# Moving one sequence's Mamba prologue from the FFN in front of its scan into the scan of the sequence ahead

## The chip, the cores and the metric

The kernel runs on one core of a Trainium2 chip. Its engines work side by side, each through its own queue of instructions in order: TensorE (PE: matmuls and transposes, with PEld for its weight loads), VectorE (DVE), ScalarE (ACT: activation functions and copies), GpSimd (POOL) and SyncE (SP: it issues most of the transfers). The metric is the time of one execution on the device, in microseconds (us).

## The reference

Sixteen sequences (B = 16) of S = 512 tokens with D = 256 channels, in float32, go through four layers with residuals: a Mamba-like selective scan, an FFN with FP4-quantized operands, a causal linear attention, and the same FFN again. Each layer sees a layernorm of its input.

```python
x = L0_attn_a_x                                                     # (16, 512, 256)
x = x + mamba(layernorm(x), w_in, w_x, w_dt, b_dt, A_log, Dp)
x = x + ffn(layernorm(x), w_gate, w_up, w_down)                     # FP4 in blocks of 16
x = x + linear_attention(layernorm(x), W_attn, b_attn, W_proj, b_proj)
x = x + ffn(layernorm(x), w_gate, w_up, w_down)

# mamba, cut to what matters
x_in = x @ w_in                                                     # u
dt_low, Bm, Cm = split(x_in @ w_x, [64, 80])
dt = softplus(dt_low @ w_dt + b_dt) * (DT_MAX - DT_MIN) + DT_MIN
A = -exp(A_log)                                                     # (256, 16)
def step(h, (dtt, ut, bt, ct)):                                     # over 512 tokens
    dA = dtt[:, :, None] * A
    inp_term = einsum('bdn,bn,bd->bn', dA, bt, ut)                  # the same for all d
    h = exp(dA) * h + inp_term[:, None, :]                          # h: (b, 256, 16)
    y = einsum('bdn,bn->bd', h, ct) + Dp * ut
```

The input term of the recurrence doesn't depend on the channel d. The state has 256 x 16 rows over 512 tokens for each sequence.

## The kernel before

**Sequences and layers.** Each sequence `b` passes through Python generators that emit instructions and yield after each piece an estimate of its length: `front` (L430), `prologue` (L444), `mamba` (L500), `ffn` (L571), `attention` (L649), `ffn` again. `weave` (L829) puts pieces of two generators side by side; `by_turns` (L867) takes from several so that each keeps to its share of a total.

**The Mamba layer.** `front` takes the layernorm's statistics of x (`bn_stats`, `bn_aggr` on VectorE, a power on POOL) and turns x to features on partitions: eight matmuls against a diagonal of the inverse deviations (L421, `pt_m`; each fp32 matmul stands as two in the profile, so sixteen), copied by ScalarE to `tT_m`. `prologue` makes everything that the scan needs, by matmuls of 128x512 from `tT_m`, four of them in the profile (two `k` steps, two records each) for each 128x512 result:

- `pz` (two halves) through Abs and Relu, then Tanh and Ln over the whole (L460 to L470) and one VectorE instruction (L471) to `dt`. Eight transfers (L476) write `dt` to DRAM as `dd`.
- `pu` (two halves), copied to `u`.
- `pcm`, copied to `cm` (C, each row repeated over eight channels).
- `dtu` = `dt` x `u` (VectorE, L485), two matmul steps to `pg` (L488); `pbm` (B) copied to one half of `inp` (L494), times `pg` (L495, VectorE), and copied to the other half (L496).

Buffers are tagged, and a tile waits until the tile before it with the same tag is read for the last time. `soft`, `dtu` and later the scan's result `yT` share one buffer (tag `soft`); `dt` and `inp` share one (tag `dt`); `u` and `cm` have one each.

`mamba` runs sixteen steps, each for two groups of 8 channels x 16 states. In a step: a transfer repeats rows of `dd` over the states (`sp`, L509, three buffers, issued two steps ahead); ScalarE makes the decay as Exp at half scale and a Square (`bar`, L521 and L524, two buffers, one step ahead); VectorE runs the scan over 2 x 512 elements (L540) and multiplies by `cm` (L544) to `h` (three buffers); PE sums over the states into `py` (L550, one PSUM bank in a pool of its own), where the skip term has been put at steps 1 and 9 (L538, from `u`). After steps 8 and 16 ScalarE copies `py` to `yT` (L555). At the end transposes and additions bring the result into x (L564, L377).

**FFN and attention.** The FFN quantizes its input on VectorE (L230 to L252), does two matmuls against resident weights (L592), the activation (L598 to L600), quantizes again in four chunks, transposes (L614) and multiplies (L627). Attention makes q and k through Exp and Relu (L670 to L672), and then in four chunks scores (L710, L717) and the products. `ko` (L681) is a copy of all of k with the even heads zeroed; each chunk's odd heads read from it.

**The order of the work.** For each round `b` from 1 to 15, the first half emits, by turns, `first(b)` up to FIRST = 76 units, and the second FFN of sequence `b - 2` with the beginning of attention `b - 1`. The second half emits the rest of `first(b)` by turns with the rest of attention `b - 1`. `first(b)` is the scan of `b`, with the front of `b + 1` from the seventh step on, and then FFN 1 of `b` with the prologue of `b + 1` among its pieces. So the last of a prologue is emitted at the end of a first half, and the scan that needs it in the next round.

The order of emission is not yet the order on the engines. The framework plans, at build time, each engine's order: emission order is the priority, and an instruction whose inputs and buffers are ready may go ahead of an earlier one that isn't. In the trace, steps of the scan of `b + 1` stand between pieces of FFN 1 of `b` that were emitted before them. All seven PSUM banks of the pool `bank` serve everything but `py`.

Of the kernel before, what the change touches and what calls it, by code (L numbers as in the profile page):

```python
# [32 lines left out]
def kernel(  # L33
# [63 lines left out]
    xs = [load(0)]  # L97
    begun, turned, stats = {}, {}, {}
    w_in_sb = const.tile([P, ND, D], F32, name="w_in_sb")
# [343 lines left out]

    def prologue(b):  # L444

        xnT = turned.pop(b)

        def from_xn(w, name):
            p = bank(f"{name}_{b}")
            for k in range(ND):  # L450
                nc.tensor.matmul(p, w[:, k], xnT[:, k, :], start=(k == 0), stop=(k == ND - 1))
            return p
# [11 lines left out]
        yield 0.5  # L464
        u = one.tile([P, ND, S], F32, tag="u", name=f"u_{b}")
        for e in range(ND):
            nc.scalar.copy(u[:, e, :], from_xn(w_in_sb[:, :, ts(e, P)], f"pu{e}"))
        yield 0.5
        nc.scalar.activation(soft, soft, AF.Tanh, scale=0.5)
# [9 lines left out]
        yield 1.5  # L479
        cm = one.tile([P, S], F32, tag="cm", name=f"cm_{b}")  # L480
        nc.scalar.copy(cm, from_xn(w_c_sb, "pcm"))


        dtu = one.tile([P, ND, S], F32, tag="soft", name=f"dtu_{b}")
        nc.vector.tensor_tensor(dtu, dt, u, ALU.mult)  # L485
        pg = bank(f"pg_{b}")
        for k in range(ND):
            nc.tensor.matmul(  # L488
                pg, a_rep[:, k].rearrange("p n i -> p (n i)"), dtu[:, k, :],
                start=(k == 0), stop=(k == ND - 1),  # L490
            )
        pb = from_xn(w_b_sb, "pbm")
        inp = one.tile([P, 2, S], F32, tag="dt", name=f"inp_{b}")
        nc.scalar.copy(inp[:, 0, :], pb)  # L494
        nc.vector.tensor_tensor(inp[:, 1, :], inp[:, 0, :], pg, ALU.mult)  # L495
        nc.scalar.copy(inp[:, 0, :], inp[:, 1, :])  # L496
        begun[b] = (u, dd, inp, cm)
        yield 2.5

    def mamba(b, xt):  # L500
        u, dd, inp, cm = begun.pop(b)

        yT = one.tile([P, ND, S], F32, tag="soft", name=f"yT_{b}")

# [25 lines left out]
        for at, (e, j, q0) in enumerate(steps):  # L530
# [5 lines left out]
            if j == 0 and q0 == 0:  # L536
                py = ps_y.tile([P, S], F32, tag="y", name=f"py_{b}_{e}")
                nc.tensor.matmul(py, d_diag[:, e], u[:, e, :], start=True, stop=False)  # L538
            h = one.tile([P, 2, S], F32, tag="hs", name=f"h_{b}_{e}_{j}_{q0}", bufs=3)
            nc.vector.tensor_tensor_scan(  # L540
# [6 lines left out]
            else:  # L547

                for q in range(4):
# [3 lines left out]
                    )  # L553
            if j == 3 and q0 == 2:
                nc.scalar.copy(yT[:, e, :], py)  # L555
            yield 3.5
# [92 lines left out]
    def attention(b, xt):  # L649
# [28 lines left out]


        ko = att.tile([P, ND, S], F32, tag="ko", name=f"ko_{b}", bufs=1)  # L680
        nc.scalar.activation(ko, kf, AF.Copy, scale=odd_heads[:, 0:1])  # L681
        yield 0.1

        def scores(c):
# [18 lines left out]
            yield 0.1  # L703

            psc = [bank(f"psc_{b}_{c}_{g}") for g in range(4)]
            for s in range(NH // 4):
                e, odd = divmod(s, 2)
                for g in range(4):
                    rows = slice(32 * g, 32 * g + (2 * HD if odd else HD))
                    nc.tensor.matmul(  # L710
                        psc[g][:, ts(s, P)], (ko if odd else kf)[rows, e, tok],
                        qf[rows, e, tok], start=True, stop=True,
                    )
# [13 lines left out]
        def attend(c, vp, sm):  # L727
# [21 lines left out]

            dx = att.tile([P, ND * HB, HD], F32, tag="dx", name=f"dx_{b}_{c}")  # L750
            nc.gpsimd.tensor_copy(
# [10 lines left out]
            if c < NC - 1:  # L762
                pk = bank(f"pk_{b}_{c}")
                for e in range(ND):
                    nc.tensor.transpose(pk[:, ts(e, P)], kf[:, e, tok], ident)
                kt = att.tile([P, D], F32, tag="kt", name=f"kt_{b}_{c}")
                nc.scalar.copy(kt, pk[:, :D])
# [69 lines left out]

    def first(b, scanned=False):

        if b + 1 < B:  # L840
            xs.append(load(b + 1))
        more = b + 1 < B
        fr = front(b + 1, xs[b + 1]) if more else iter(())
        if not scanned:
            yield from weave(mamba(b, xs[b]), fr, 6)
        yield from fr
        yield from weave(ffn(0, "f", b, xs[b]), prologue(b + 1) if more else iter(()), 0)

# [5 lines left out]

    FIRST, CHUNKS, FRONT, ATTN, FFN2 = 76.0, 30.0, 4.15, 23.0, 40.0

# [22 lines left out]
    with tc.tile_pool(name="prep", bufs=3) as prep, tc.tile_pool(name="prep_m", bufs=1) as prep_m:  # L879
        weights = ffn_weights(prep)  # L880
        next(weights)
        composite_weights(prep_m)
        for _ in weave(front(0, xs[0]), weights, 1, False):
            pass
        for _ in weave(prologue(0), weights, 0, False):
            pass
        for _ in weave(mamba(0, xs[0]), weights, 0):
            pass
    att = ctx.enter_context(tc.tile_pool(name="att", bufs=2))
    acts.append(ctx.enter_context(tc.tile_pool(name="act1", bufs=1)))  # L890
    by_turns([(first(0, True), CHUNKS)])
    for b in range(1, B):
# [40 lines left out]
```

## Time and profile before

The median of three runs is 2849.44 us (2849.22 to 2851.41). All below is of one profiled execution.

| | |
|---|---|
| profiled execution, its own time | 2856.84 us |
| its span, first to last instruction | 2855.1 us |
| mean granted TensorE clock | 0.929 of full |
| first scan instruction of sequences 1, 2, 3, 4 | 148.4, 260.1, 442.6, 610.6 us |
| rounds from sequence 3 to 15 | 167.3 to 170.6 us each |
| from the first to the last scan of one sequence, rounds 4 to 14 | 104 to 107 us |
| last scan instruction of sequence 15 ends | 2571 us |
| VectorE: scans and multiplies of the Mamba layer | 581.6 + 310.7 us |
| PE: reducing matmuls of the Mamba layer | 284.7 us |
| share of the 16 DMA engines, main queue | 22.0% |

Rounds repeat almost to the nanosecond from sequence 3 on, so one of them can be read for all. A table of stretches gives, for each stretch, the busy time of every engine; what an engine lacks to the length of the stretch is its idle time. The waits name who stood still, at which line, and what ended the wait. The chain of waits goes back from the last instruction to what released each one; what lies on it sets the time, and work that lies beside it costs nothing.

### The profile page before, as it was taken

The numbers are of one execution on the slowest core, as the hardware profiler recorded it, in microseconds if no ns is written. First come the engines' busy times: TensorE is split into PE (matmuls) and PEld (weight loads), VectorE is DVE, ScalarE is ACT, GpSimd is POOL, SyncE is SP. The second block draws the span as 40 slices with busy tenths as digits, with TensorE's granted clock in tenths as the row PEclk, the third lists the DMA queues.
The fourth block names the chain that finished last, engine by engine and source line by source line (L and its number), as shares of the span: only waits on it lengthen the run. The fifth ranks groups of instructions, "written<-read, shape, count | busy, mean of one in ns | idle before, by whom it ended". The sixth has DMA issues, their size and how long they took to land.

```text
span 2855.1 us, 34186 instructions
## 1 busy us (share of the span) xinstructions
PE 2450.1 (86%) x12907; PEld 1451.0 (51%) x12907; DVE 2433.6 (85%) x3545; ACT 1493.4 (52%) x2798; POOL 154.6 (5%) x153
## 2 busy tenths in 40 slices
PE   6577989898988889898898989989898888988997
PEld 3143555454554545455554545545455454545664
DVE  7797888989798898979888898888979889897565
ACT  4666455555545555554555555555554555553322
POOL 2000000000000000000000000000000000000000
PEclk7788999999999999999999999999899999999988
DMA  5332104132230313213031320403222041320000
GB/s 146 89 96 74 52 1 106 36 82 60 56 73 13 102 39 82 60 38 89 15 96 45 82 60 9 110 23 85 56 59 74 8 103 38 74 59 7 2 1 15
DMA packets 64376, 165.26 MB, mean 58 GB/s; under 512 B 8434, under 2 KB 26836, under 8 KB 64212
## 3 DMA queue, kind: packets, MB, share of 16 engines
q1 hardware_dynamic: 62592, 162.03, 22.0%
q8 instruction: 101, 1.65, 0.2%
q10 hardware_dynamic: 1620, 1.06, 0.1%
q14 instruction: 63, 0.52, 0.1%
HBM read 146.28 MB, written 16.78 MB: 57 GB/s over the span
## 4 chain that ended last, share of the span: by engine, by line
DVE 45%; PE 38%; ACT 8%; issue 6%; POOL 2%; DMA 0%; SPq 0%; ACTq 0%; DVEq 0%; POOLq 0%
DVE h L540 15%; PE po_g L627 5%; DVE h L544 5%; PE pg_g L592 4%; PE pu_g L592 4%; PE pqk L664 3%; DVE sm L717 3%; PE po_f L627 3%; PE pu_f L592 2%; PE pg_f L592 2%; DVE amax_f L230 2%; PE py L550 2%; DVE v_f L244 2%; DVE h_f L600 2%; DVE x L377 1%
## 5 line engine op out<-in xcount | busy, mean ns | idle before, releaser
L540 DVE TENSOR_TENSOR_SCAN h<-bar,inp 128x1024 f32<-128x1024 f32 x256 | 581.6, 2281 | 31.8 <-ACT inp L496 22.4
L521 ACT ACTIVATE bar<-sp,a_col 128x511 f32<-128x511 f32 x512 | 348.6, 715 | 287.6 <-DVE h L540 278.9
L550 PE MATMUL py<-h,red 128*32 128x512 f32 x1024 | 284.7, 712 | 111.6 <-DVE h L544 111.6
L544 DVE TENSOR_TENSOR h<-h,cm 128x1024 f32<-128x1024 f32 x256 | 310.7, 1214 | 1.0
L524 ACT ACTIVATE bar<-bar 128x1022 f32<-128x1022 f32 x256 | 269.8, 1054 | 5.6
L627 PE MATMUL po_f<-wdT,hqT_f 128*128 128x256 f32 (+1 forms) x768 | 205.8, 412 | 24.8 <-ACT hqT_f L618 24.8
L627 PE MATMUL po_g<-wdT,hqT_g 128*128 128x256 f32 (+1 forms) x768 | 200.1, 403 | 31.4 <-ACT hqT_g L618 31.4
L627 PEld LDWEIGHTS po_f<-wdT,hqT_f 128*128 128x128 f32 (+1 forms) x768 | 142.7, 199 | 120.3 <-ACT hqT_f L618 61.3
L592 PE MATMUL pg_f<-wgT,tT_f 128*128 128x352 f32 x512 | 191.3, 498 | 12.8 <-DVE sm L717 9.5
L592 PE MATMUL pu_f<-wuT,tT_f 128*128 128x352 f32 x512 | 178.5, 472 | 18.7 <-DVE sm L717 18.4
L627 PEld LDWEIGHTS po_g<-wdT,hqT_g 128*128 128x128 f32 (+1 forms) x768 | 138.6, 193 | 92.0 <-ACT hqT_g L618 45.2
L592 PE MATMUL pg_g<-wgT,tT_g 128*128 128x352 f32 x512 | 178.3, 471 | 0.0
L592 PE MATMUL pu_g<-wuT,tT_g 128*128 128x352 f32 x512 | 173.2, 460 | 0.0
L717 DVE TENSOR_TENSOR sm<-psc,causal 128x512 f32<-128x512 f32 x256 | 162.9, 676 | 5.4 <-PE psc L710 4.1
L248 ACT ACTIVATE big_f<-v_f 128x704 bf16<-128x704 f32 (+1 forms) x80 | 67.4, 842 | 166.9 <-DVE v_f L244 166.3
L592 PEld LDWEIGHTS pu_f<-wuT,tT_f 128*128 128x128 f32 x512 | 99.2, 196 | 80.9 <-DVE sm L717 25.7
L550 PEld LDWEIGHTS py<-h,red 128*32 128x32 f32 x1024 | 35.7, 116 | 203.6 <-DVE h L544 171.1
L592 PEld LDWEIGHTS pg_g<-wgT,tT_g 128*128 128x128 f32 x512 | 94.9, 191 | 73.4 <-issue 33.4
L592 PEld LDWEIGHTS pg_f<-wgT,tT_f 128*128 128x128 f32 x512 | 92.8, 197 | 76.1 <-issue 17.7
L592 PEld LDWEIGHTS pu_g<-wuT,tT_g 128*128 128x128 f32 x512 | 97.8, 191 | 54.7 <-issue 1.0
L664 PE MATMUL pqk<-tT_a,w_qkv_sb 128*128 128x512 f32 x256 | 125.1, 617 | 0.0
L598 ACT ACTIVATE h_g<-pg_g 128x352 f32<-128x352 f32 x128 | 59.0, 461 | 95.6 <-PE pg_g L592 94.8
(235 smaller groups left out, 4614.7 us busy)
## 6 DMA issues: line engine op xcount, KB each, us to landing
sp<-dd SPq DMA_DIRECT2D x256, 512.0 KB, 4.7
x<-in_L_attn_a_x_dram SPq DMA_DIRECT2D x16, 512.0 KB, 5.0
dd<-dt SPq DMA_DIRECT2D x128, 64.0 KB, 1.7
out_dram<-x SPq DMA_DIRECT2D x16, 512.0 KB, 4.5
w_qkv_sb<-in_L_attn_b_W_attn_dram ACTq DMA_DIRECT2D x1, 768.0 KB, 7.2
raw_d<-in_L_ffn_w_down_dram SPq DMA_DIRECT2D x1, 704.0 KB
raw_g<-in_L_ffn_w_gate_dram SPq DMA_DIRECT2D x1, 640.0 KB, 7.2
raw_u<-in_L_ffn_w_up_dram SPq DMA_DIRECT2D x1, 640.0 KB, 6.5
```

What stands on the lines that cost most here:

```text
L230: nc.vector.tensor_reduce(amax, src.rearrange("p (b k) -> p b k", k=BLK), AX.X, ALU.max, apply_absolute_value=True,)
L248: nc.scalar.activation(big, v, AF.Abs, scale=STEP)
L521: nc.scalar.activation(bar[:, i, 1:S], sp[:, i, 1:S], AF.Exp, scale=a_col[:, g : g + 1])
L524: nc.scalar.activation(bar[:, :, 1:S], bar[:, :, 1:S], AF.Square)
L540: nc.vector.tensor_tensor_scan(h.rearrange("p i t -> p (i t)"), bar.rearrange("p i t -> p (i t)"), inp.rearrange("p i t -> p (i t)"), 0.0, ...
L544: nc.vector.tensor_tensor(h, h, cm.unsqueeze(1).to_broadcast([P, 2, S]), ALU.mult)
L550: nc.tensor.matmul(py[32 * q : 32 * q + 32, :], red[:, j, :], (h0, h)[q // 2][:, q % 2, :], start=False, stop=(j == 3),)
L592: nc.tensor.matmul(pw[:, :HF], xqT[:, k, ts(c, P)], wT[:, k, cols], start=(k == 0), stop=(k == ND - 1),)
L598: nc.scalar.activation(hc, pg[:, :HF], AF.Tanh, scale=0.5)
L627: nc.tensor.matmul(po[:, :D], hqT[:rows, r, :], wdT[:rows, r, :], start=(r == 0), stop=(r == NR - 1),)
L664: nc.tensor.matmul(pz, w_qkv_sb[:, k, ts(je, P)], xnT[:, k, :], start=(k == 0), stop=(k == ND - 1),)
L717: nc.vector.tensor_tensor(t, psc[g].rearrange("p (s t) -> p s t", t=P), causal.unsqueeze(1).to_broadcast([P, NH // 4, P]), ALU.mult,)
```

## The change

- `prologue(b + 1)` now begins with `front(b + 1)`, and both are emitted among the steps of the scan of `b` (from its second step on) in place of the FFN. What follows the scan in `first(b)` is FFN 1 alone. The startup does the same with sequences 0 and 1.
- Within `prologue`, `pu` and `u` move behind `cm`. From there on it emits nothing until the scan ahead has emitted step 9, whose matmul is the last reader of `u` (the counter `halfway`).
- `dtu` is gone: `dt` is multiplied by `u` in place. B goes into `dt`'s first half (`term`), times `pg` there.
- `inp` has a buffer of its own. `mamba` fills it at its beginning: one half by ScalarE, one by POOL. Before, ScalarE wrote both within the prologue.
- `cm` has two buffers. `yT` is taken from the `soft` buffer only after step 8.
- In attention `ko` is made for each chunk (128x256 four times instead of 128x1024 once), and `dx` and `kt` have one buffer instead of two.
- The units FIRST and FRONT become 74.0 and 4.1.

```diff
-    def prologue(b):
-
+    def prologue(b, xt):
+
+        yield from front(b, xt)
         xnT = turned.pop(b)
...
         yield 0.5
-        u = one.tile([P, ND, S], F32, tag="u", name=f"u_{b}")
-        for e in range(ND):
-            nc.scalar.copy(u[:, e, :], from_xn(w_in_sb[:, :, ts(e, P)], f"pu{e}"))
-        yield 0.5
         nc.scalar.activation(soft, soft, AF.Tanh, scale=0.5)
...
-        cm = one.tile([P, S], F32, tag="cm", name=f"cm_{b}")
+        cm = one.tile([P, S], F32, tag="cm", name=f"cm_{b}", bufs=2)
         nc.scalar.copy(cm, from_xn(w_c_sb, "pcm"))
-
-
-        dtu = one.tile([P, ND, S], F32, tag="soft", name=f"dtu_{b}")
-        nc.vector.tensor_tensor(dtu, dt, u, ALU.mult)
+        yield 0.1
+
+        while halfway[0] < b:
+            yield 0
+        u = one.tile([P, ND, S], F32, tag="u", name=f"u_{b}")
+        for e in range(ND):
+            nc.scalar.copy(u[:, e, :], from_xn(w_in_sb[:, :, ts(e, P)], f"pu{e}"))
+        yield 0.5
+
+        nc.vector.tensor_tensor(dt, dt, u, ALU.mult)
         pg = bank(f"pg_{b}")
         for k in range(ND):
             nc.tensor.matmul(
-                pg, a_rep[:, k].rearrange("p n i -> p (n i)"), dtu[:, k, :],
+                pg, a_rep[:, k].rearrange("p n i -> p (n i)"), dt[:, k, :],
                 start=(k == 0), stop=(k == ND - 1),
             )
-        pb = from_xn(w_b_sb, "pbm")
-        inp = one.tile([P, 2, S], F32, tag="dt", name=f"inp_{b}")
-        nc.scalar.copy(inp[:, 0, :], pb)
-        nc.vector.tensor_tensor(inp[:, 1, :], inp[:, 0, :], pg, ALU.mult)
-        nc.scalar.copy(inp[:, 0, :], inp[:, 1, :])
-        begun[b] = (u, dd, inp, cm)
-        yield 2.5
+        term = dt[:, 0, :]
+        nc.scalar.copy(term, from_xn(w_b_sb, "pbm"))
+        nc.vector.tensor_tensor(term, term, pg, ALU.mult)
+        begun[b] = (u, dd, term, cm)
+        yield 2

     def mamba(b, xt):
-        u, dd, inp, cm = begun.pop(b)
-
-        yT = one.tile([P, ND, S], F32, tag="soft", name=f"yT_{b}")
+        u, dd, term, cm = begun.pop(b)
+
+        inp = one.tile([P, 2, S], F32, tag="inp", name=f"inp_{b}")
+        nc.scalar.copy(inp[:, 0, :], term)
+        nc.gpsimd.tensor_copy(inp[:, 1, :], term)
...
                 nc.tensor.matmul(py, d_diag[:, e], u[:, e, :], start=True, stop=False)
+                if e == ND - 1:
+                    halfway[0] = b + 1
...
             if j == 3 and q0 == 2:
+                if e == 0:
+                    yT = one.tile([P, ND, S], F32, tag="soft", name=f"yT_{b}")
                 nc.scalar.copy(yT[:, e, :], py)
...
-        ko = att.tile([P, ND, S], F32, tag="ko", name=f"ko_{b}", bufs=1)
-        nc.scalar.activation(ko, kf, AF.Copy, scale=odd_heads[:, 0:1])
-        yield 0.1
...
+            ko = att.tile([P, ND, P], F32, tag="ko", name=f"ko_{b}_{c}")
+            nc.scalar.activation(ko, kf[:, :, tok], AF.Copy, scale=odd_heads[:, 0:1])
...
-    def first(b, scanned=False):
+    def scan(b):

         if b + 1 < B:
             xs.append(load(b + 1))
-        more = b + 1 < B
-        fr = front(b + 1, xs[b + 1]) if more else iter(())
-        if not scanned:
-            yield from weave(mamba(b, xs[b]), fr, 6)
-        yield from fr
-        yield from weave(ffn(0, "f", b, xs[b]), prologue(b + 1) if more else iter(()), 0)
+            yield from weave(mamba(b, xs[b]), prologue(b + 1, xs[b + 1]), 1)
+        else:
+            yield from mamba(b, xs[b])
+
+    def first(b):
+
+        yield from scan(b)
+        yield from ffn(0, "f", b, xs[b])
...
-    FIRST, CHUNKS, FRONT, ATTN, FFN2 = 76.0, 30.0, 4.15, 23.0, 40.0
+    FIRST, CHUNKS, FRONT, ATTN, FFN2 = 74.0, 30.0, 4.1, 23.0, 40.0
...
-        for _ in weave(front(0, xs[0]), weights, 1, False):
+        for _ in weave(prologue(0, xs[0]), weights, 2, False):
             pass
-        for _ in weave(prologue(0), weights, 0, False):
-            pass
-        for _ in weave(mamba(0, xs[0]), weights, 0):
+        for _ in weave(scan(0), weights, 0):
             pass
...
-    by_turns([(first(0, True), CHUNKS)])
+    by_turns([(ffn(0, "f", 0, xs[0]), CHUNKS)])
```

More of the change, by code (lines that the diff above doesn't have):

```diff
@@ L97 @@
     xs = [load(0)]
-    begun, turned, stats = {}, {}, {}
+    begun, turned, stats, halfway = {}, {}, {}, [0]
     w_in_sb = const.tile([P, ND, D], F32, name="w_in_sb")
@@ L710, in scores @@
                     nc.tensor.matmul(
-                        psc[g][:, ts(s, P)], (ko if odd else kf)[rows, e, tok],
+                        psc[g][:, ts(s, P)], ko[rows, e, :] if odd else kf[rows, e, tok],
                         qf[rows, e, tok], start=True, stop=True,
@@ L748, in attend @@
             nc.scalar.copy(num, pn)
-            dx = att.tile([P, ND * HB, HD], F32, tag="dx", name=f"dx_{b}_{c}")
+            dx = att.tile([P, ND * HB, HD], F32, tag="dx", name=f"dx_{b}_{c}", bufs=1)
             nc.gpsimd.tensor_copy(
@@ L765, in attend @@
                     nc.tensor.transpose(pk[:, ts(e, P)], kf[:, e, tok], ident)
-                kt = att.tile([P, D], F32, tag="kt", name=f"kt_{b}_{c}")
+                kt = att.tile([P, D], F32, tag="kt", name=f"kt_{b}_{c}", bufs=1)
                 nc.scalar.copy(kt, pk[:, :D])
```

## The prediction

> **What bounds the kernel now.** I read the page's busy shares first:
>
> ```profile
> PE 2450.1 (86%) x12907; PEld 1451.0 (51%) x12907; DVE 2433.6 (85%) x3545; ACT 1493.4 (52%) x2798; POOL 154.6 (5%) x153
> ```
>
> Two engines, TensorE (PE) and VectorE (DVE), share the span almost evenly, so neither alone is the bound. From the start of one sequence's scan to the next is a round, 167 to 171 us. Busy time in one round, and in its two stretches (columns: us, then PE, PE weight load, DVE, ACT, POOL busy with their counts, granted clock, DMA):
>
> ```profile
> 945.30:1112.90 167.60, 146.09 (x804) 87.19 (x803) 149.44 (x219) 92.27 (x174) 9.05 (x8) 0.97 0.23 60
> 945.30:1050.00 104.70, 86.72 (x585) 51.65 (x584) 101.71 (x139) 58.11 (x109) 8.05 (x7) 0.95 0.26 71
> 1050.00:1112.90 62.90, 59.37 (x220) 35.54 (x219) 47.73 (x81) 34.16 (x65) 1.01 (x1) 1.00 0.17 42
> ```
>
> Stretch A, with the sixteen scan steps, is DVE's: 97.1% busy, while PE leaves 18.0 us unused. Stretch B, without scans, is PE's: 94.4% busy, while DVE leaves 15.2 us. B ends in the prologue, as VectorE's waits say (us in total, times, longest), and as the chain of waits shows at the end of this round:
>
> ```profile
> DVE inp L495 <- ACT inp L494: 69.2, 13, 5.5
> DVE h L540 <- ACT inp L496: 22.4, 14, 2.0
> ...
> 1104.67 1.91 PE pcm L451 x4
> 1106.58 1.72 PE pg L488 x4
> 1108.30 1.73 PE pbm L451 x4
> 1110.05 0.59 ACT inp L494
> ```
>
> The next scan stands ready but for `inp`; `inp` needs twelve matmuls that PE reaches only behind the FFN's. DVE stands 5.3 us, then 1.6 us, in nearly every round.
>
> **The change, part by part, per round.**
>
> *PE moved from B to A*: pz 8, pu 8, pcm 4, pg 4, pbm 4 matmuls of 128x512. Four take 1.72 us in the chain, so 28 take 12.1 us. The front's 16 transposing matmuls (pt_m, 1.8 us) move within the round; I count nothing for them. B keeps 59.4 - 12.1 = 47.3 us of PE; A gets 86.7 + 12.1 = 98.8.
>
> *DVE moved*: L471 1.21, L485 1.22, L495 0.69: 3.1 us. B keeps 44.6, A gets 104.8.
>
> *ACT moved*: Abs and Relu 2.7, Tanh 1.06, Ln 1.15 with two table loads of 1.28, u 1.16, cm 0.58, one inp copy 0.6: 9.8 us, so A has 67.9 in about 108.
>
> *The sum before extras*: A at its own DVE share is 104.8 / 0.971 = 107.9; B at its own PE share is 47.3 / 0.944 = 50.1; together 158.0 against 167.6, **9.6 us less a round**. The cover is DVE in A: PE's gaps lie beside its work. Were that cover gone, the 12.1 us would be on the path again and nothing won.
>
> *Extras, 2.1 us a round*:
> - The Ln and its table loads now stand among the decays, 3.7 us in a row, with 2.1 us of Tanh and Relu near by. Two decay buffers cover up to two steps of 3.5 us. Bounds 0 and 3.7; I take 1.0, near the trace's row for such a wait (0.5 us in this round). The Trainium skill ("ScalarE: Activation LUTs", What ACT_TABLE_LOAD costs) puts a switch at 2.66 us, its load and a drain of 1.38. In this trace Ln starts at 1093.76, right behind a load of 1.28 from 1092.46, so the drain doesn't show. By the rule the row of ACT work would be 6.5 us, just within the cover, and the term 2 to 3: some 20 us more over the kernel.
> - POOL now copies half of `inp` (128x512) at each hand-over. The nearest row is dx, 128x256 at 0.40 us unhindered and at most 1.30. By its size I take 0.65, up to 3 behind a scan, partly under other DVE work: 0.6. The Trainium skill ("SBUF — State Buffer", SBUF: two separate sides) says that a POOL instruction and a DVE one with two SBUF inputs exclude each other for the whole instruction. A scan reads two. By that, DVE loses up to 0.65 a round, 10 us in all; in the trace the longest of 256 scans is 2.38 us against 2.28, and it is the one beside a dx, so 0.1 a round, 1.5 us in all. I take the row.
> - ko per chunk: four ACT copies of some 0.37 (the 128x256 copy's row) for one of 1.15, +0.3 on ACT, and the first lies ahead of the odd scores: 0.4. `dx` and `kt` with one buffer: POOL is 5% busy and the chunks are in sequence; 0, at most 0.4.
> - SP: the eight dd writes (3.7 us of issue) now stand ahead of this scan's sp loads, and wait for dt. In this scan an sp load is issued 18 to 42 us before its step from the fourth step on; landing takes 4.7 and the decay 2.5, so 11 us are to spare: 0. Lateness of dt beyond 11 us would come through, step by step.
> - New waits: `u` waits for the second half's d_diag matmul (L538); behind it on ACT stand the decays. The order of issue puts it after that matmul, so 0. `yT` waits for `soft`, now the next sequence's: see the slow rival.
>
> So 7.5 us a round. Rounds 3 to 14 are alike: 12 x 7.5 = 90. Earlier, from the end of scan 0 to the start of scan 2 (115 to 260 us) DVE is busy 108.3 of 145.1; scan 1 can start at once there, and I halve the 36.8 idle: 18. The round from 260 to 442 idles 29.4, and I bring it to 20, that of later rounds: 9. At the end, scans drawn forward leave less to fill the last FFNs with: +8, between 0 and 17 (one B stretch's idle is 15). Sum 90 + 18 + 9 - 8 = 109. The profiled execution took 2856.8 (span 2855.1), so 2747.8; the runs' median lies 7.4 lower: **2740 us**, 3.8% less.
>
> **Rivals.**
>
> *PE sets the end* (chance 0.22). PE's 18 us in A are in small pieces: its waits for h are 6.2 us in 5 pieces, longest 3.1. A group of four matmuls needs 1.7. If half of the group work fits, about half of the 6.9 us of visible wait is won, 3.5 a round: 42 + 9 + 4.5 - 8 = 47.5, **2802**. For it: PE has no gap of note at the boundary. Against: PE's queue may run behind a little without anyone waiting, seven banks deep.
>
> *Scans fill everything* (0.08). With the next scan ready throughout B, DVE keeps A's share everywhere: 149.4 / 0.971 = 153.9 a round, 13.7 less; 164 + 33 + 25 - 8 = 214: **2635**. Against: PE would need 95% as well.
>
> *Slower: dt late for the buffer that yT shares* (0.17). Place: `soft`, one buffer, held by the next sequence from pz until L471 is done; then yT of this scan's first half. ACT's copy of py into yT waits for it; behind it the only py bank, the second half's d_diag and reducing matmuls on PE, the three h buffers, and the scans. Deadline: step 8 is at 53.8, its sums by about 59. The next x lands about 12 us after the scan's start (issued at 1120.0, 5.0 to landing). The chain unhurried: statistics 2.3, var and power 2.0, diag 1.6, transposes 1.8, copies 1.1, pz 3.4, Abs/Relu 1.3, Tanh 1.1, load and Ln 2.4, L471 1.2: 18 us, so dt at 30 and 29 us to spare. For the rival: before, statistics at 980 and transposes at 1059 lay 78 us apart, since nothing pressed them. It decides from 29 + 7.5 = 37 us of delay on. At 12 us late: 12 - 7.5 = 4.5 a round over 13 rounds, 59 more: **2908**.
>
> *Nothing moves* (0.03): each engine's order follows a plan made at build time, issue order being only its priority; if that plan leaves the scan where it is, 2849.
>
> **How the numbers follow.** The forecast has 0.50. Its own range, 2695 to 2790, is rounds 3.5 us better or worse; the low-clock rounds differ by that much (170.6 at 0.93 granted, 167.3 at 0.97). Faster: 0.50 + 0.22 + 0.08 = 0.80; same (within 0.2%, about what these runs can tell) 0.03; slower 0.17. The 80% range runs from 2655, leaving out half of the 0.08, to 2860, leaving out nearly all of the 0.17.
>
> **What would show it.** Right: no wait of DVE for `inp` L494; pz to pbm among the scans; the next scan's first step inside what was B; rounds of 158 to 162 us; DVE and PE both at 89 to 91%. PE the bound: PE's idle stays near 20 us a round, and DVE's gaps turn into waits for PE. Slow rival: ACT's yT copy or PE's d_diag waits long, and SP stands at the dd writes with sp loads behind. Wrong altogether if the plan spreads the prologue so that scans of the second half wait.

## The result and the profile after

The changed kernel took **3013.61 us** (median of four, 3011.59 to 3016.86) against 2849.33 (2844.91 to 2851.41): a ratio of 1.058, 95% interval 1.0561 to 1.0598. The forecast was 2740 with a range to 2860, so both the value and the range were wrong, and the sign too.

The busy shares of the page after the change:

```profile
PE 2463.3 (82%) x12907; PEld 1464.3 (49%) x12907; DVE 2451.0 (81%) x3545; ACT 1507.3 (50%) x2846; POOL 144.7 (5%) x169
```

And the table of stretches for one round, scan start to scan start (us, then PE, weight load, DVE, ACT, POOL busy with counts, granted clock, DMA share, GB/s):

```profile
1338.60:1516.10 177.50, 147.61 (x803) 88.47 (x803) 150.50 (x220) 93.15 (x177) 7.98 (x9) 0.95 0.22 57
```

The engines do the same work as before (DVE 2451 against 2434 us, PE 2463 against 2450); a round is 177.5 us instead of 167.6, and what was added is idle time of both: 29.9 us of PE and 27.0 of DVE, against 21.5 and 18.2 in the round shown before. That rules out the two rivals in which an engine is full; nor is it a lower clock that costs, since PE's busy time is nearly the same. Counted from the times at which each x is written out, 129 us of the 157 us of longer span lie in the fifteen rounds between the first and the last write-out, and 28 before the first one, where the prediction had a gain of 27.

The scan does start early: of VectorE's waits for `inp` 1.6 us are left in all. But its steps are now spread over 174.5 us of the round of 177.5, where they took 105 before, with 60 us without a scan step between the eleventh and the twelfth. VectorE's waits after (us in total, times, longest), and the row of the first of them before:

```profile
DVE qk L679 <- ACT ep L678: 164.1, 31, 11.7
DVE h_f L606 <- ACT h_f L605: 76.8, 67, 2.7
```

```profile
DVE qk L672 <- ACT ep L671: 65.2, 29, 4.3
```

The wait for `inp` (69.2 and 22.4 us before) is gone, and VectorE stands instead at the hand-over to the attention, where FFN 1 of a sequence has ended and its attention begins, beside the second FFN of the sequence ahead: 99 us more in sixteen rounds. It also stands longer for ScalarE inside FFN 1 (`h_f`, 23.2 us before). The timeline of PE after, there (start, length, and in brackets what it waited):

```profile
1454.18 2.05 PE L421 MATMUL pt_m<-diag_m,x 128*128 128x128 f32 x16
...
1458.55 2.05 PE L421 MATMUL pt_a<-diag_a,x 128*128 128x128 f32 x16 [2.32 <-ACT diag_a L414]
1460.44 3.60 PE L452 MATMUL pz<-tT_m,w_z_sb 128*128 128x512 f32 x8
1463.88 1.04 PE L419 MATMUL pt_g<-ident,xn_g 128*128 128x128 f32 x8
1464.75 1.88 PE L671 MATMUL pqk<-tT_a,w_qkv_sb 128*128 128x512 f32 x4
```

And VectorE's timeline beside it:

```profile
1457.23 1.22 DVE L252 TENSOR_TENSOR xn_g<-v_g,half_g 128x1024 f32<-128x1024 f32 x1
1468.45 0.69 DVE L679 SCALAR_TENSOR_TENSOR qk<-ep 128x512 f32<-128x512 f32 x1 [10.00 <-ACT ep L678]
...
1471.27 1.23 DVE L468 SCALAR_TENSOR_TENSOR dt<-soft,dt 128x1024 f32<-128x1024 f32 x1 [1.06 <-ACT soft L467]
```

The prologue's products haven't gone into TensorE's small gaps among the scans. They stand in front of the products that open the attention and the second FFN, while VectorE has nothing else to do for 10 us. ScalarE's part of the prologue stands there too, in front of `ep`, for which VectorE waits:

```profile
1462.36 0.69 ACT L461 ACTIVATE soft<-pz,b_dt_sb 128x512 f32<-128x512 f32 x1 [1.13 <-PE pz L452]
...
1466.18 1.09 ACT L466 ACTIVATE soft<-soft 128x1024 f32<-128x1024 f32 x1
1467.14 0.71 ACT L677 ACTIVATE ep<-pqk,b_qk_sb 128x512 f32<-128x512 f32 x1
```

No run here takes ScalarE's part away, so how the 10 us divide between the two engines is open. The front was ready long before: ScalarE makes the last of `diag_m` at 1388.75, 65 us ahead of the transposes. The second place is FFN 1's head, the layernorm and quantizing with which it begins. PE's timeline after, there, and VectorE's:

```profile
1534.80 1.54 PE L621 MATMUL pt_h_g<-ident,h_g 128*128 128x128 f32 x6 [7.74 <-DVE h_g L252]
1536.34 1.92 PE L555 MATMUL py<-h,red 128*32 128x512 f32 x4
1538.19 3.54 PE L634 MATMUL po_g<-wdT,hqT_g 128*128 128x256 f32 x12
1545.57 1.50 PE L555 MATMUL py<-h,red 128*32 128x512 f32 x4 [3.84 <-DVE h L549]
1547.00 1.97 PE L419 MATMUL pt_f<-ident,xn_f 128*128 128x128 f32 x8
```

```profile
1529.65 1.21 DVE L230 TENSOR_REDUCE amax_f<-xn_f 128x64 f32<-128x1024 f32 x1
...
1531.68 2.28 DVE L545 TENSOR_TENSOR_SCAN h<-bar,inp 128x1024 f32<-128x1024 f32 x1
...
1537.33 4.47 DVE L545 TENSOR_TENSOR_SCAN h<-bar,inp 128x1024 f32<-128x1024 f32 x2
...
1545.43 1.22 DVE L252 TENSOR_TENSOR xn_f<-v_f,half_f 128x1024 f32<-128x1024 f32 x1
```

Scan steps of the next sequence now stand between the pieces of FFN 1's quantizing on VectorE, and TensorE stands idle 7.74 and 3.84 us for VectorE. In the kernel before, `pz` and `pu` lay at this place. From the first `xn_f` to the transposes `pt_f` it takes 20 us, against 13.6 before.

### The profile page after: what moved, and what is told of

It is laid out like the page before. It is cut to its first block, busy times and chain, and to the rows that moved or that the text cites. A ratio compares the mean times of both kernels' runs of the same rounds, so it can differ in the third digit from the quotient of the medians.

```text
span 3012.4 us, 34256 instructions
## 1 busy us (share of the span) xinstructions
PE 2463.3 (82%) x12907; PEld 1464.3 (49%) x12907; DVE 2451.0 (81%) x3545; ACT 1507.3 (50%) x2846; POOL 144.7 (5%) x169
## 4 chain that ended last, share of the span: by engine, by line
DVE 49%; PE 31%; ACT 10%; issue 6%; POOL 2%; DMA 0%; DVEq 0%; SPq 0%; ACTq 0%; POOLq 0%
DVE h L545 13%; PE po_f L634 7%; DVE h L549 4%; PE pg_f L599 3%; PE pu_f L599 3%; PE po_g L634 3%; DVE sm L722 2%; DVE v_g L250 2%; DVE v_f L250 2%; DVE v_f L251 2%; DVE v_f L244 2%; DVE v_g L251 2%; PE pz L452 2%; PE py L555 2%; DVE h_g L252 1%
## 5 line engine op out<-in xcount | busy, mean ns | idle before, releaser
L634 PE MATMUL po_f<-wdT,hqT_f 128*128 128x256 f32 (+1 forms) x768 | 220.4, 434 | 68.6 <-ACT hqT_f L625 68.6
L634 PE MATMUL po_g<-wdT,hqT_g 128*128 128x256 f32 (+1 forms) x768 | 208.8, 416 | 22.5 <-ACT hqT_g L625 22.5
L634 PEld LDWEIGHTS po_f<-wdT,hqT_f 128*128 128x128 f32 (+1 forms) x768 | 152.7, 213 | 139.7 <-ACT hqT_f L625 93.1
L634 PEld LDWEIGHTS po_g<-wdT,hqT_g 128*128 128x128 f32 (+1 forms) x768 | 145.0, 202 | 96.7 <-ACT hqT_g L625 36.9
L599 PE MATMUL pg_f<-wgT,tT_f 128*128 128x352 f32 x512 | 182.1, 479 | 0.2 <-ACT tT_f L425 0.2
L679 DVE SCALAR_TENSOR_TENSOR qk<-ep 128x512 f32<-128x512 f32 x64 | 44.0, 688 | 164.1 <-ACT ep L678 164.1
L621 PE MATMUL pt_h_g<-ident,h_g 128*128 128x128 f32 (+1 forms) x384 | 69.7, 322 | 117.8 <-DVE h_g L252 117.8
L621 PEld LDWEIGHTS pt_h_g<-ident,h_g 128*128 128x128 f32 (+1 forms) x384 | 47.6, 155 | 178.3 <-DVE h_g L252 141.6
L606 DVE SCALAR_TENSOR_TENSOR h_f<-h_f,pg_f 128x352 f32<-128x352 f32 x128 | 66.1, 517 | 76.8 <-ACT h_f L605 76.8
```

The source lines that it names most:

```text
L599: nc.tensor.matmul(pw[:, :HF], xqT[:, k, ts(c, P)], wT[:, k, cols], start=(k == 0), stop=(k == ND - 1),)
L621: nc.tensor.transpose(pt[:rows, ts(r - r0, P)], h[:, r * P : r * P + rows], ident)
L634: nc.tensor.matmul(po[:, :D], hqT[:rows, r, :], wdT[:rows, r, :], start=(r == 0), stop=(r == NR - 1),)
```

## The experiments

The expectations name theories by letters. **A**: dt is late for the buffer that yT shares, the prediction's slow rival. **B**: the prologue's products at the hand-over, in front of those of the attention and the second FFN, are the cost. **C**: the scan's early start is the cost, since it takes VectorE from FFN 1's head. **D**: in the new order of emission FFN 1's head lies away from the matmuls of the second FFN, which should fill TensorE beside it. **E**: before, the prologue's products fill TensorE while VectorE quantizes for FFN 1; moved, they leave that place bare and stand at the hand-over. Two runs test whether the prologue stands too late in TensorE's order. All ratios are to the kernel before, beside its own runs.

### Theory A, and the order on TensorE

**own_yT**: the first half of yT gets a buffer of its own (with one buffer of `ko` to make room).

```diff
-                if e == 0:
-                    yT = one.tile([P, ND, S], F32, tag="soft", name=f"yT_{b}")
-                nc.scalar.copy(yT[:, e, :], py)
+                yT = one.tile([P, S], F32, tag="soft" if e else "yT0", name=f"yT_{b}_{e}")
+                nc.scalar.copy(yT, py)
+                yTs.append(yT)
...
```

> The changed kernel, but yT's first half has a buffer of its own (2 KB; the second half stays with soft, and ko has one buffer, to make room). Theory A (the scan is cut in two because yT waits for the next sequence's soft): the 62 us without a scan step between steps 11 and 12 go, the 10 us in which VectorE waits for q and k are filled with scans, a round falls from 177.5 us to 160 to 168, and the time to 2750 to 2860. Theory B (the prologue's matmuls in front of attention's and the second FFN's first matmuls are what costs): they stay where they are, so a round stays at 172 or more, and the time at 2930 to 3010.

2982.38 us, ratio 1.0431 (1.0399 to 1.0462). The scan's steps draw together (127 to 134 us), but VectorE's wait at the hand-over is still 131.7 us. The sharing accounts for 1.5 of the 5.8 per cent here; theory A expected 2860 or less, theory B 2930 to 3010.

**earlier_rank**: the pieces of the prologue get a higher priority in the plan.

```diff
+        with tc.high_priority(offset=800):
             soft = one.tile([P, ND, S], F32, tag="soft", name=f"soft_{b}")
...
```

> The changed kernel, with every instruction of the prologue ranked 800 instructions (about a round) earlier in the plan's priority. If the transposes stand 65 us after their inputs are ready because the FFN and attention rank ahead of them, they go forward to about 50 us after the scan's start, and the time falls to 2850 or less. If they stand there because PSUM banks are handed out in the order of issue, the rank changes nothing: 2990 to 3030.

3133.03 us, ratio 1.096 (1.0931 to 1.0989), slower than either case expected. `diag_m` is made 16 us earlier in the scan, and `pt_m` begins 76 us behind it, where it was 67 in the change: priority doesn't free the transposes. What makes this kernel slower wasn't looked into.

**own_bank**: the prologue's products and transposes get a PSUM bank of their own, and six stay for the rest.

```diff
-    ps = ctx.enter_context(tc.tile_pool(name="ps", bufs=7, space=PSUM))
+    ps = ctx.enter_context(tc.tile_pool(name="ps", bufs=6, space=PSUM))
+    ps_p = ctx.enter_context(tc.tile_pool(name="ps_p", bufs=1, space=PSUM))
...
```

> The changed kernel, but the prologue's matmuls write to a PSUM bank of their own, and the others have six instead of seven. soft is still shared with yT. If banks in the order of issue held the transposes back, they now run among FFN 1 and the scans, dt is ready some 50 us earlier, step 12 is no longer 62 us behind step 11 (20 or less), and the time is 2760 to 2880. If not: 3000 to 3060, with one bank less to work in.

2997.16 us, ratio 1.0485 (1.0457 to 1.0513), outside both cases. Now `pt_m` and `pz` do go forward, in among FFN 1 and the attention: `pt_m` begins 51 us into the scan instead of 116, and 0.4 us behind `diag_m` instead of 67. So it is the bank that held them: the seven banks are given out in order of emission, and the products can't pass those emitted ahead of them, while scan steps, whose `py` has a bank of its own, can. In the change `pt_m` is emitted behind the scan's third step and runs 116 us behind its first. A place among the emitted scan steps is therefore no place among the executed ones. The pause before the twelfth step shrinks from 60 to 25 us; by itself the bank is worth 1 per cent.

**buffers_only**: the kernel before with all side parts of the change (buffers, `term`, POOL's copy, `ko` by chunk), and the prologue where it was.

```diff
-        inp = one.tile([P, 2, S], F32, tag="dt", name=f"inp_{b}")
+        term = dt[:, 0, :]
...
+        nc.gpsimd.tensor_copy(inp[:, 1, :], term)
```

> The kernel before with the rest of the change alone: inp in its own buffer with POOL's copy, dt times u in place, cm in two, yT taken at step 8, ko per chunk, dx and kt with one buffer; front and prologue stay where they were. All theories: within 15 us of 2849, since none of it lies on the path; over 2880 would mean that a side part costs.

2872.82 us (11 runs), ratio 1.0059 (1.0044 to 1.0074). The side parts cost 17 us by themselves. VectorE's wait for `inp` has only changed its name:

```profile
DVE dt L493 <- ACT dt L492: 81.2, 16, 7.8
```

### Theory C: the scan held back

**yT_hold**: own_yT, with the first scan step issued only behind the last addition of the second FFN of sequence b - 3; **yT_hold_mid**: behind its second one; **hold_only**: the changed kernel with the first hold alone; **all_three**: own_yT, own_bank and the hold.

```diff
+            ins = ends.get((b - 3, 3)) if at == 0 else None
+            with tc.issue_after(ins) if ins else nullcontext():
                 nc.vector.tensor_tensor_scan(
```

> yT's first half in its own buffer as in own_yT, and the first scan step of each sequence is kept in VectorE's order behind the last addition of the second FFN three sequences earlier, which is where the kernel before begins its scan. The prologue stays among the scan's steps. Theory C (the scan starts 27 to 43 us too early: its steps then lie beside a stretch in which VectorE is full anyway, and none are left for the hand-over to the next FFN and attention, where VectorE stands idle): a round falls to 163 to 170, the time to 2800 to 2890. Theory B (the prologue's matmuls stand in front of the hand-over's): nothing is moved there, so 2940 or more.

2984.51 us, ratio 1.048 (1.0464 to 1.0495).

> The same, but held only behind the second of that FFN's four additions, some 20 us earlier. Theory C: between own_yT and yT_hold, 2870 to 2950. Theory B: as own_yT, 2960 to 2990.

2968.88 us, ratio 1.0412 (1.0377 to 1.0447).

> The changed kernel with the hold alone; yT still shares soft with the next sequence. Theory C says that the early start costs, and sharing adds its own: dt is ready only some 110 us after the scan's start, steps 9 and later wait for it, so 2950 to 3060. If sharing costs nothing of its own, as yT_hold, 2800 to 2890.

3056.77 us, ratio 1.0732 (1.0716 to 1.0748).

> yT's first half in its own buffer, the prologue's matmuls in a bank of their own, and the hold. Theory C alone: within 30 us of yT_hold. If the prologue's place at the hand-over costs as well (theory B in part), another 30 to 80 us faster than yT_hold, down to 2760; one bank less for the others may take some of it back.

2921.62 us, ratio 1.026 (1.0242 to 1.0277). To hold the scan back gives at most 0.2 per cent (yT_hold_mid against own_yT, within the intervals), so its early start isn't by itself the cost. yT_hold, yT_hold_mid and all_three lie where theory B put them, hold_only where C put it if the sharing costs as well. All three together take off 3.2 per cent, more than the 1.5 and 1.0 of the first two; what they do to one another wasn't split. With the hold, the shared buffer costs 2.5 per cent instead of 1.5.

### Theory D: TensorE's order

**before_late_ffn**: the kernel before, with the first half weighed 68 instead of 76, so that FFN 1 falls later against the second FFN.

```diff
-        halves = [(some(new, FIRST), FIRST)]
+        halves = [(some(new, FIRST), 68.0)]
```

> The kernel before, with one number changed: in the first half of a round, first(b) takes turns with a weight of 68 in place of 76, so that FFN 1 begins when the second FFN beside it is 90% emitted instead of 80%, as in the changed kernel (65.7 of 74 units lie ahead of it there). FFN 1's first transposes then stand behind the last matmuls of the other FFN instead of among them. Theory D (what costs in the change is that FFN 1's layernorm and quantizing no longer lie beside the other FFN's matmuls, since the prologue counts 8 units in the turns): 5 to 9 us a round more, 2910 to 2990. If the prologue's matmuls at the hand-over (theory B) or the scan's start are what costs: within 20 us of 2849.

2891.84 us, ratio 1.0146 (1.0125 to 1.0166): 42 us, less than expected, but the place of FFN 1 has a price in the kernel before as well.

**turns**: the changed kernel with the prologue's pieces counted at nothing, FIRST 68 and a weight of 72, so that FFN 1 falls again where it was against the second FFN; **turns_yT**: with own_yT; **turns_yT_bank**: with own_bank too.

```diff
-            yield from weave(mamba(b, xs[b]), prologue(b + 1, xs[b + 1]), 1)
+            free = (0 for _ in prologue(b + 1, xs[b + 1]))
+            yield from weave(mamba(b, xs[b]), free, 1)
...
-        halves = [(some(new, FIRST), FIRST)]
+        halves = [(some(new, FIRST), 72.0)]
```

> The changed kernel, with the prologue's pieces counted as 0 in the turns and first(b) taking turns with 72 for 68 units, so that FFN 1 begins at 80% of the other FFN, as before. soft is still shared. Theory D: 5 to 9 us a round less than the changed kernel, 2870 to 2940. Theory B: 2990 or more.

3076.02 us, ratio 1.0799 (1.0783 to 1.0815).

> The same turns, and yT's first half in its own buffer. Theory D with the sharing's 30 us: 2840 to 2910. Theory B: 2960 or more, as own_yT.

2933.87 us, ratio 1.0298 (1.0283 to 1.0313).

> The same turns, yT's first half in its own buffer, and the prologue's matmuls in a bank of their own, so that they leave the hand-over. If both D and B cost: 2770 to 2850, at or below the kernel before. If D alone: as turns_yT within 25 us. If B alone: 2900 to 2940.

2900.45 us, ratio 1.0173 (1.0154 to 1.0193). With yT's buffer free, the order is worth 1.3 per cent and the bank another 1.25. With yT's buffer shared, the same order is worse than the change itself: there the sharing alone costs 5.0 per cent. Its price is no fixed one; that it depends on how far dt comes behind the scan's middle is a guess. The sums of theory D for turns and turns_yT were missed, and turns_yT_bank lies at the edge of what was given for B alone. Nor do the turns bring back the order alone: VectorE stands 122.0 us for `soft` ahead of dt in both kernels, against 24.2 in the change.

### Theories C and E against each other

**turns_yT_s6** and **turns_yT_s12**: turns_yT with the prologue woven in from the scan's seventh and thirteenth step; **turns_yT_bank_hold**: turns_yT_bank with the hold.

```diff
-            yield from weave(mamba(b, xs[b]), free, 1)
+            yield from weave(mamba(b, xs[b]), free, 6)
```

> The kernel of turns_yT (half of yT in a buffer of its own, the prologue's pieces counted at nothing, the first half of the other work so long that TensorE's order is kept) with the prologue woven in from the scan's step 7 on instead of from its step 2. TensorE then has the transposes of x and the z product behind the attention's transposes and q/k products instead of in front of them, and C, gate and B among FFN 2's products. Theory E (the time went because the prologue's products no longer stand beside FFN 1's quantizing, and stand at the other hand-over instead): the hand-over to the attention comes free, FFN 1's head stays bare, so 2890 to 2920 us, below turns_yT's 2934 (2849 before). Theory C (the scan's early start, which takes VectorE from FFN 1's head, is the cost): the scan starts as early as in turns_yT, so 2925 to 2945.

3017.2 us, ratio 1.0594 (1.0578 to 1.061).

> As turns_yT_s6, woven in from the scan's step 13 on, so that the x transposes and the z product stand in TensorE's order close ahead of FFN 1's head, near where they stand in the kernel before, and the last four steps of the scan are issued among them. Theory E: 2860 to 2890 us, close to buffers_only (2873), and faster than turns_yT_s6. Theory C: no faster than turns_yT_s6 by more than 10 us as long as the next scan begins before FFN 1's quantizing.

3065.78 us, ratio 1.0764 (1.0746 to 1.0782). Both are slower than turns_yT, by 83 and 132 us: a miss for both theories. PE's timeline of turns_yT_s12 shows a new wait:

```profile
1512.27 3.60 PE L452 MATMUL pu<-tT_m,w_in_sb 128*128 128x512 f32 x8
...
1529.50 3.78 PE L491 MATMUL pg<-dt,a_rep 128*128 128x512 f32 x4 [7.94 <-DVE dt L488]
```

Between `pu` and `pg` lies the chain over `u` and dt on ScalarE and VectorE. Before, TensorE had FFN 1's first chunk between them; here it stands 7.94 us, and all behind `pg` stands with it. In turns_yT_s6 PE waits 89.7 us in all for dt at `pg`, in turns_yT_s12 130.8, in turns_yT 17.1. So these two don't test the place alone, and don't tell C from E.

> turns_yT_bank (2900 us), with the first step of each scan issued only behind the last addition of the second FFN three sequences back, so that no scan of the next sequence lies beside FFN 1's normalizing and quantizing. Theory C (the early scan slows FFN 1's head, its removal gives the time back): 2850 to 2885. Theory E (the head is bare on TensorE either way, and what was done early is now done late): 2895 to 2950.

3013.33 us, ratio 1.0579 (1.0564 to 1.0595), 113 us slower than without the hold. Theory C falls, and the price is above what E gave. The longest of PE's waits:

```profile
PE pt_f L424 <- DVE xn_f L257: 184.9, 15, 13.5
```

And FFN 1's head in the table of stretches:

```profile
1497.60:1509.60 12.00, 1.49 (x5) 0.45 (x3) 11.07 (x20) 1.40 (x2) 1.65 (x1) 0.68 0.01 1
```

With neither the prologue nor a scan beside it, TensorE stands 12.3 us a round at FFN 1's head, at a clock of 0.68, and these waits are 120.6 us longer in all than in turns_yT_bank, about the 113 us lost. In the kernel before, the rounds of sequences 3 to 14 have no such wait. That the prologue covered it there, and the early scan covers it in part after the change, is how these rows read; the hold moves the scan's other steps as well.

**before_c_last**: the kernel before, with C's products and copy moved behind B's, since C isn't needed for the first scan.

```diff
-        cm = one.tile([P, S], F32, tag="cm", name=f"cm_{b}")
-        nc.scalar.copy(cm, from_xn(w_c_sb, "pcm"))
...
         nc.scalar.copy(inp[:, 0, :], inp[:, 1, :])
+        cm = one.tile([P, S], F32, tag="cm", name=f"cm_{b}")
+        nc.scalar.copy(cm, from_xn(w_c_sb, "pcm"))
```

> The kernel before with one thing moved: the four products of C and the copy of C stand behind those of the gate and of B, since C is wanted only after the first scan step and B and the gate ahead of it. In the kernel before, the scan waits some 5 us a round for inp. If that wait sets the end of the hand-over, 1.9 us (four products) to 2.5 us come off in each of 15 rounds: 2810 to 2825 us. If TensorE's total work there sets it, nothing: 2845 to 2853. A slower time than 2855 is expected by neither.

2844.82 us (median of 20 runs), ratio of the means 1.0004 (0.9992 to 1.0017): no difference. VectorE's two waits for `inp` did shrink, from 69.2 and 22.4 us, but its wait for the decay, 9.3 us before, grew:

```profile
DVE inp L490 <- ACT inp L489: 46.6, 13, 3.6
DVE h L537 <- ACT bar L521: 45.0, 14, 3.3
...
DVE h L537 <- ACT inp L491: 2.0, 3, 0.8
```

The three together went from 100.9 to 93.6 us. In the kernel before, ScalarE makes the first decay's Exp ahead of `pbm` (Exp at 1107.10, `inp` at 1110.05); here `inp` is copied first, at 1112.38, and the Exp stands behind it, at 1112.86. So one wait was exchanged for another, and what a scan that really starts earlier would win here isn't tested. The scan stood ready but for `inp` and, close behind, the decay.

### What the moved matmuls are worth at the old and the new place

**before_less_pe** and **after_less_pe**: 18 of the prologue's 28 matmuls (by the profile's count) are left out, in the kernel before and in the changed one; each product keeps its first half of the features alone, and z and u are made for one half of the channels and copied twice.

```diff
-            for k in range(ND):
-                nc.tensor.matmul(p, w[:, k], xnT[:, k, :], start=(k == 0), stop=(k == ND - 1))
+            nc.tensor.matmul(p, w[:, 0], xnT[:, 0, :], start=True, stop=True)
...
+        pz = from_xn(w_z_sb[:, :, ts(0, P)], "pz0")
         for e in range(ND):
-            pz = from_xn(w_z_sb[:, :, ts(e, P)], f"pz{e}")
...
```

> The kernel before, with 18 of the prologue's 28 matmuls left out and nothing put elsewhere: each product keeps its first half of the features alone, and z and u are computed for one half of the channels and copied twice (so values are not the reference's; every copy, activation, transfer and wait stays). TensorE does 18 x 0.43 = 7.7 us less a round, all of it in stretch B. The prediction's step (B ends when TensorE's share of 94.4% is done, so matmuls taken out of B shorten the round by their time): 8.2 us in each of 15 rounds, 123 us: 2720 to 2735 us. Theory E (B is as long as the chain of FFN 1's head on VectorE and of dt; the prologue's products only fill TensorE's time beside it): a third of it at most, 2805 to 2850 us.

2878.28 us, ratio 1.0103 (1.0085 to 1.012): with 7.7 us of matmuls less in every round, the kernel is 29 us **slower**. Outside what either theory gave, and the prediction's step falls outright. Where the matmuls were, TensorE now waits; the row in the kernel before, where its three waits lie at 135, 246 and 2618 us, outside the regular rounds, and in before_less_pe:

```profile
PE pt_f L419 <- DVE xn_f L252: 39.1, 3, 15.5
PE pt_f L419 <- DVE xn_f L252: 154.6, 16, 14.7
```

The 24 us of FFN 1's head, from 132 to 156 us behind a write-out of x, in the kernel before:

```profile
1416.80:1440.80 24.00, 21.33 (x76) 12.06 (x74) 21.29 (x41) 16.51 (x31) 1.01 (x1) 1.00 0.07 18
```

PE's timeline there:

```profile
1434.08 1.12 PE L538 MATMUL py<-u,d_diag 128*128 128x512 f32 x2 [1.00 <-ACT u L467]
1435.18 1.09 PE L419 MATMUL pt_f<-ident,xn_f 128*128 128x128 f32 x8
1436.52 1.45 PE L592 MATMUL pg_f<-wgT,tT_f 128*128 128x352 f32 x4 [0.24 <-ACT tT_f L425]
```

The same stretch in before_less_pe, and PE's timeline in it:

```profile
1428.30:1452.30 24.00, 14.00 (x44) 8.20 (x43) 20.01 (x31) 13.41 (x22) 1.01 (x1) 0.79 0.28 67
```

```profile
1437.80 1.12 PE L537 MATMUL py<-u,d_diag 128*128 128x512 f32 x2 [1.06 <-ACT u L467]
1447.87 1.97 PE L419 MATMUL pt_f<-ident,xn_f 128*128 128x128 f32 x8 [8.94 <-DVE xn_f L252]
1449.66 2.38 PE L591 MATMUL pg_f<-wgT,tT_f 128*128 128x352 f32 x4
```

PE does 7.3 us less in these 24, and `pt_f` comes no earlier: it waits 8.94 us for VectorE, which is busy over 80% of the stretch in both kernels. Then PE runs at a lower clock: 1.97 us for 1.09 and 2.38 for 1.45, 1.8 us in two rows. Over the whole kernel PE is busy 2354.3 us, 96 less than before, though 124 us of matmuls are gone: some 28 us, 1.8 a round, went to the lower clock. A round takes 170.7 us instead of a mean of 168.8 (167.3 to 170.6), 1.9 more. One more thing differs, as read from VectorE's timeline: the plan now puts the quantizing of a chunk of the second FFN among FFN 1's, so that `pt_f` is 1.2 us later. The two weren't separated.

> The changed kernel with the same 18 matmuls left out, at the place to which it moves them. The prediction's step (TensorE is idle 18 us in stretch A and takes them there for next to nothing): 3000 to 3014 us. Theory E (they lie at the hand-over to the attention, ahead of its transposes and q/k products, which VectorE waits for): their time comes back, 7.7 us in each of 15 rounds, 116 us: 2890 to 2930 us. In between: theory E has a part.

2978.15 us, ratio 1.0453 (1.0438 to 1.0469): 35 us come back, 2.4 us a round of the 7.7, between the two expectations. But the page shows that PE is as busy as in the change (2463.3 us), with 288 matmuls less:

```profile
PE 2464.4 (83%) x12619; PEld 1471.2 (49%) x12619; DVE 2448.8 (82%) x3545; ACT 1507.2 (51%) x2846; POOL 159.7 (5%) x169
```

The mean granted clock fell from 0.915 to 0.872, and the other matmuls took longer by about what was left out. So the moved matmuls aren't free at their new place, but what they cost there by themselves this run doesn't tell. ScalarE's part of the prologue stays in it, and VectorE still stands 141.1 us for `ep`, against 164.1.

## Why the prediction was wrong

**"B at its own PE share 47.3 / 0.944 = 50.1"**: this step failed first, and the forecast stood on it. A busy share of 94.4% was taken for a bound. before_less_pe took 7.7 of the 12.1 us out of B and moved nothing elsewhere: by the step 8.2 us a round are won, measured were 1.9 lost, and without the 1.8 us that the lower clock took it would have been about nothing. The wait behind the prologue's products was there all along: PE waits for VectorE at `pt_f` as soon as they are gone. The chain of waits says so too, further up than the four lines that the prediction shows of it:

```profile
1082.95 0.73 DVE xn_f L402 x2
...
1091.04 1.06 ACT big_f L248
...
1096.56 0.65 PE pt_f L419 x4
```

So B is as long as the chain through FFN 1's head and dt lets it be, and the prologue's products were cover for it. That this chain is the bound is read from the traces; no run shortens it. Of VectorE's 15.2 idle us in B little lies there: in the 24 us of FFN 1's head shown above it is idle for 2.7.

**"The next scan stands ready but for `inp`"** left out the decay, which came close behind (before_c_last), and of the "twelve matmuls" four are C's, which `inp` doesn't need. (Seven groups of 1.72 us are 12.0, not 12.1; it changes nothing.)

**"The cover is DVE in A"** and **"dt at 30 and 29 us to spare"**: the products were to run where they are emitted, and these steps failed as well. dt was made at 1472.5, 134 us behind the scan's start, since banks are given out in order of emission (own_bank), and the prologue ran at the hand-over, in front of what VectorE waits for. I had the number that speaks against it, 78 us between statistics and transposes before, and put it down to nothing pressing them.

**The slow rival** had its place right: after the change the first half's yT is copied at 1474.05, 135 us into the scan, where it was 72 before (1017.68, not "about 59"), and the scan stands still for 60 us. The third sign says nothing: SP stands 651 us in all at the dd writes, but 1036 before. Its size was wrong: at 12 us of lateness 59 us over the kernel before was forecast; measured are 63 us of lateness, and the sharing costs 42 by the ratios of own_yT and the change (31 by their medians), 72 with the hold and 143 with the turns. It is a part and not the cause.

**"I count nothing for" pt_m** and **the end +8** weren't isolated. **The start** (18 + 9 us of gain) turned into a loss of 28. **The extras**: 2.1 us a round, and buffers_only measured 0.59%, 17 us, or 1.1 a round, without what the move itself brings to them.

By the ratios, from the kernel before to the change (of 2849 us):

| step | ratio | us |
|---|---|---|
| side parts (buffers_only) | 1.0059 | 17 |
| prologue moved, with order, bank and yT's buffer kept (turns_yT_bank) | 1.0173 | 32 |
| without a bank of its own (turns_yT) | 1.0298 | 36 |
| without TensorE's order (own_yT) | 1.0431 | 38 |
| with yT's buffer shared (the change) | 1.0580 | 42 |

The order of the steps has a say in their size, as the sharing shows. The second row is open: in turns_yT_bank PE waits about 4 us for FFN 1's rows in nearly every round, where there was no such wait before, which fits theory E but is a reading; the runs meant to isolate it brought waits of their own. Why TensorE's order (fourth row) costs what it does is open too: the runs show only that it does. No version here beat the kernel before.

## What to carry to other kernels

An engine that is 94% busy in a stretch isn't shown to be its bound: ask what it would stand at if its work were gone, and try it by leaving work out before moving it, with an eye on the clock, which can take back what was left out. Work that looks like a burden may be the cover of another engine's chain, and it leaves a hole where it was. The place in which a piece is emitted is not where it runs: look for the resource that is given out in order, here the PSUM banks, and see how far other streams run ahead of it.

## What the hardware showed

Taking matmuls away made the matmuls behind them slower. In three stretches in which PE stands for 7 us and more, its granted clock is down: 0.66 in the 7 us at FFN 1's head after the change, 0.68 in the 12 us of turns_yT_bank_hold, 0.79 in the 24 us of before_less_pe, where eight transposes then take 1.97 us for 1.09. The stretch after the change:

```profile
1526.80:1533.80 7.00, 0.26 (x2) 0.00 (x0) 7.00 (x11) 0.79 (x1) 0.00 (x0) 0.66 0.00 0
```

The Trainium skill ("TensorE: Matmul & The Clock Gate", Part 1) has the clock halved after an idle window of about 3.4 us, until a window is busy again. The rows agree: with 8.94 us idle the clock fell, and after the 1.00 us gap before `py` in the kernel before it stayed at 1.00. Filler on PE so keeps the clock up as well: without it before_less_pe loses 1.8 us a round in the two rows above, and in after_less_pe the lower clock takes back all of the 124 us of matmuls left out.
